# A channel-attention and dilated-attention kernel: softmax weights turned by TensorE, taps summed three at a time, attention loads cut to 32 rows

## The chip, the cores and the metric

One Trainium2 chip, one of its cores. The metric is the device time of the whole program in microseconds (us), as the median of the runs shown. About 0.3% is what a measurement of this kernel can tell from no change.

The engines are called as in the profile: PE (TensorE, matrix products), PEld (its weight loads), DVE (VectorE), ACT (ScalarE), POOL (GpSimd), SP (which here only issues transfers). POOL also issues transfers; those that add to their target in flight are all issued by POOL.

## The reference

The input x is 4 images of 192 channels of 128 x 128 pixels, in float32. Two layers follow each other.

```
# layer 0: attention between channels
qkvl = dwconv3x3(conv1x1(x, w_qkv), w_dw)            # 4 x 192 channels
q, k, v, l = split(qkvl, 4)                           # 8 heads of 24 channels
q, k = q / norm(q), k / norm(k)                       # over all pixels
attn = softmax(q @ k.T * temperature)                 # 24 x 24 for each head and image
out  = attn @ v
L    = silu(fc2(relu(fc1(mean(l)))))                  # one number for each channel
x    = conv1x1(L + out + x, w_proj) + L

# layer 1: attention between neighbouring pixels
x    = x + dwconv3x3(x, pos_w) + pos_b
q, k, v = conv1x1(x, qkv_w)                           # 3 groups of 64 channels, dilation 1, 2, 3
for g in groups:                                      # 2 heads of 32 channels in a group
    scores = q . k at the 9 dilated neighbours (reflected at the border)
    out[g] = softmax(scores / sqrt(32)) weighted sum of v at the 9 neighbours
y    = conv1x1(concat(out), proj_w)
```

## The kernel before, in words

The program has three stages. **Projection** (`project`) makes the q and k channels of layer 0, stores them to memory (`qk_dram`), and makes the convolved v (`v_dram`, `v2_dram`). **Channel attention** (`channel_attention`) reads q and k back row by row, convolves them on PE with banded 32 x 32 tap matrices and forms the small attention matrices, already multiplied with the projection (`mix1`, `mix2`). **The second pass** (`second_pass`) does the rest: it forms layer 0's output h, and from it the whole of layer 1.

Projection and second pass work in 64 blocks: pairs of images (2) by four rows of pixels (32). A tile is 128 partitions by `PX` = 512 pixels. In the second pass a block goes through these steps, with the names of the code:

- `h_product`, `h_evict` (L1081, L1085): h, 128 channels of each image, and the last 64 channels of both images in one tile; written into rings of 12 rows (`hboth`, `hring`).
- `centre`, `tap` (L1121, L1133): the 3 x 3 convolution of the first 128 channels, both images in one instruction of 1024 elements. The middle tap goes from ACT to a PSUM tile `pa`; DVE adds six taps (`SUMMED`). The other two (`MOVED`) are made by ACT (`moved`, L1146), added to each other and then to the tile `y` by two transfers that POOL issues (`moved_sum`, L1158). `moved` has one buffer.
- `side`, `side_rows`, `side_sum`: the same for the last 64 channels, by ACT, two adding transfers and POOL.
- `kv_product` (L1235, L1238), `kv_evict`: k and v, into rings for each dilation.
- `query` (L1292, L1295): q of one group, in one PSUM tile. Its second half is one matmul with a 128 x 128 block matrix (`wq2`).
- `prod` (L1303): DVE, q times k for three taps at once (1536 elements), nine in a block.
- `pick_sums` (L1314), `evicted_scores`, `by_pixel` (L1363): PE sums over channels, and turns the scores so that pixels lie on partitions.
- `top` to `part2` (L1366 to L1396): softmax, and the weights split into three bfloat16 parts that sum to float32.
- `weights` (L1401): a transposing transfer from SP brings them back to tap-on-partition, into `e_sb`.
- `expand` (L1436): PE spreads the weights of one tap over its 32 channels, a bfloat16 matmul of 108 rows with 512 columns, into a PSUM tile `ex` (two buffers); 27 in a block.
- `term` (L1442): DVE multiplies it with v; 27 in a block, of 512 elements.
- `term_sum` (L1445): POOL adds the terms; 24 in a block, of 512 elements.
- `out_product` (L1454, L1458), `out_evict`, `store`: the last projection. For channels 128 up it uses a 128 x 128 block matrix (`wo2`).

The order on every engine is fixed before the program runs. `Schedule` simulates the five engines and a sixth, DMA, with the cost that each `add` states; among the ready operations of an engine it takes the one of lowest rank, where rank is the block number plus a figure from `PLACES`. A change of the PE's tile shape (the `shape` of an `add`) costs `change` in the simulation and `change_rank` in the choice. `hold` says how many tiles of a kind may live at once. The engines run their queues in that order, waiting on semaphores.

In channel attention, SP and PE follow the order of the code. For each of 48 steps t (eight channels of a head) `Rows.load` has SP issue one load of small tap tables (`few`) and ten row loads of 64 or 32 partitions (`PIECES`); POOL then copies the taps into three banded matrices. `cut_taps` and `cut_loaded` load what is needed at the borders between 32-row strips, also on SP. The steps of `gates` (the L branch) are taken during head 0.

Of the kernel before, what the change touches and what calls it, by code (L numbers as in the profile page):

```python
# [29 lines left out]
NS = NG * NT * 4  # L30
GT = NT * 4
# [121 lines left out]
PIECES = (((0, 2), (2, 2)), ((0, 2), (2, 1), (3, 1)), ((0, 2), (2, 2)), ((0, 1), (1, 2), (3, 1)))  # L153
LAST = [(e, r, n) for e in range(4) for r, n in PIECES[e] if r + n == 4]
OTHERS = [(e, r, n) for e in range(4) for r, n in PIECES[e] if r + n < 4]


class Rows:
# [14 lines left out]
    def load_taps(self, t):  # L173
        first, j = self.place(t)
        few = self.few[t] = self.few_p.tile([STRIP, 4, 2, 3, STRIP], F32, tag="few", name=f"few{t}")
        self.nc.sync.dma_start(
            few.rearrange("p e c x m -> p e (c x m)"),
            self.bands_in[:, first : first + CH0]
            .rearrange("p (e c) x m -> p e (c x m)", e=4)[:, :, j * 3 * STRIP : (j + 2) * 3 * STRIP],
        )  # L180

    def spread_taps(self, t, i):

        band, few = self.bands[t % 3], self.few[t]
        group = slice(i * STRIP, (i + 1) * STRIP)
        self.nc.gpsimd.tensor_copy(band[group, :, :, :, 1 : STRIP - 1], few[:, :, :, :, 1 : STRIP - 1])  # L186
        for e, m in ((i, 0), ((i + 1) % 4, STRIP - 1)):
            self.nc.gpsimd.tensor_copy(band[group, e, :, :, m : m + 1], few[:, e, :, :, m : m + 1])  # L188
# [17 lines left out]
    def load(self, t):  # L206
        if t >= 6 * HEADS0:
            return
        self.load_taps(t)
        self.load_rows(t, OTHERS + LAST)  # L210
        for i in range(4):
            self.spread_taps(t, i)
# [49 lines left out]
def rows3(t):  # L262
# [10 lines left out]
SECOND = "wp1 wq1 wq2 wkv wkv2 wo wo2 posw posb pick order spread".split()  # L273
SUMMED, MOVED, TAPS = (0, 1, 2, 6, 7, 5), (3, 8), 0.075
# [58 lines left out]
    "loads": (0.5697, 0),  # L333
    "h_product0": (-0.8250, 0),
    "h_evict0": (0.7179, 0),
    "h_product1": (-0.2901, 0),
    "h_evict1": (4.5043, 0),
    "h_product2": (-0.7755, 0),
    "h_evict2": (-0.2139, 0),
    "centre": (5.7183, 0),  # L340
    "tap": (2.8884, 0.19030),
    "moved": (-0.0827, 0),
    "moved_sum0": (3.1492, 0),
    "moved_sum1": (4.7398, 0),
    "side1": (1.2593, 0.00003),
    "side0": (0.7171, 0.00011),
    "side_rows0": (2.1868, 0),
    "side2": (1.6271, 0.00019),
    "side_rows2": (1.4785, 0),
    "side_sum1": (10.8296, 0),  # L350
    "side_sum2": (5.4172, 0),
    "kv0": (1.7866, 0.00185),
    "kvev0": (-0.0330, 0.01478),
    "kv1": (3.2540, 0.00019),
    "kvev1": (-2.0029, 0),
    "kv2": (2.4499, 0),
    "kvev2": (1.1258, 0),
    "query0": (2.8659, 0),
    "prod0": (2.9696, 0),
    "query1": (3.3887, 0),  # L360
    "prod1": (3.0988, 0),
    "query2": (3.4244, 0),
    "prod2": (3.5942, 0),
    "pick0": (3.5728, 0.17857),
    "pick1": (3.9636, 0),
    "evicted_scores": (1.8388, 0),
    "by_pixel": (3.8163, 0),
    "top": (6.6680, 0),
    "below": (5.0643, 0),
    "exponential": (10.6231, 0),  # L370
    "total": (-2.1855, 0),
    "divide": (3.8560, 0),
    "part0": (-5.1709, 0),
    "rest": (-2.3314, 0),
    "part1": (-0.0711, 0),
    "part2": (1.6351, 0),
    "weights": (12.2563, 0),
    "expand": (4.2596, 0),
    "term": (4.7246, 0),
    "term_sum": (8.9696, 0),  # L380
    "out0": (6.1072, 0.00004),
    "outev0": (6.1953, 0),
    "store0": (18.8924, 0),
    "out1": (6.1208, 0),
    "outev1": (7.1247, 0),
    "store1": (9.7231, 0),
# [3 lines left out]
def channel_attention_then_dilated_attention(ctx: ExitStack, tc: tile.TileContext, d, out: bass.AP):  # L390
# [23 lines left out]
    with ExitStack() as early:  # L414
        band_p, u_p, few_p = (
            early.enter_context(tc.tile_pool(name=n, bufs=k)) for n, k in (("pab", 1), ("pau", 2), ("pax", 1))
        )
        rows = Rows(nc, d["bands"], qk_dram, few_p, band_p, u_p, lent)
        dwv = load(band_p, "dwv")
# [19 lines left out]
        project(tc, x, load, loads, dwv, sums, qk_dram, v_dram, v2_dram)  # L439
# [9 lines left out]
def project(tc, x, load, other_loads, dwv, sums, qk_dram, v_dram, v2_dram):  # L449
# [4 lines left out]
    with ExitStack() as ctx:  # L454
# [9 lines left out]
        plan_projection(nc, stage, x, wx, wx2, dwv, vboth, ring, sums, qk_dram, v_dram, v2_dram)  # L464
# [5 lines left out]
def plan_projection(nc, stage, x, wx, wx2, dwv, vboth, ring, sums, qk_dram, v_dram, v2_dram):  # L470
# [130 lines left out]
    load_ops, pairs = {}, {}  # L601

    def plan_products(n):
# [9 lines left out]
        for mt in range(4):  # L613
# [11 lines left out]
            hold("us", evs[0], add("SP", at(f"qkst{mt}", n), 0.3, (qk_store, n, mt), evs, latency=5.0))  # L625
# [47 lines left out]
    for n in range(2 * NB + 1):  # L673
        if n < 2 * NB:
            plan_products(n)
        if n >= 1:
            plan_conv(n - 1)

# [59 lines left out]
def channel_attention(tc, d, load, qk_dram, mix1, mix2, rows, gates):  # L738
# [7 lines left out]
    with ExitStack() as ctx:  # L746
        pool = lambda n, k, **kw: ctx.enter_context(tc.tile_pool(name=n, bufs=k, **kw))
# [6 lines left out]
        def bank(name, shape):  # L754
            taken.append(name)
            of = ps_x if len(taken) % 7 == 0 else ps_c
# [40 lines left out]
        def cut_taps(hd):  # L797
            taps = cut_p.tile([128, 2, 3, STRIP], F32, tag="taps", name=f"cuttaps{hd}")
            nc.sync.dma_start(taps, d["cuttaps"][:, hd])
            return taps  # L800

        def cut_loaded(hd, edge):
            u = cut_p.tile([128, 2, B * W], F32, tag=f"u{edge}", name=f"cut{hd}_{edge}")
            first = (edge + 1) * STRIP - 2
            for which in range(2):
                for h in range(2):
                    c0 = which * C + hd * CH0 + h * (CH0 // 2)
                    nc.sync.dma_start(
# [40 lines left out]
        def cut_squares(hd, edge, cut, sums):  # L849
            square = st.tile([128, B, 2, 2 * CH0], F32, tag="square", name=f"square{hd}_{edge}")  # L850
# [7 lines left out]
        def products(hd, q, sq, k, sk, us, taps):  # L858
# [3 lines left out]
            for b in range(B):  # L862
# [19 lines left out]
                if b == 1:  # L882
                    for edge in range(3):
                        cuts.append(cut_turned(hd, edge, s_cuts[edge]))
                        cut_squares(hd, edge, cuts[edge], (sq, sk))
# [75 lines left out]
        pending, mixes = [gate(ps_s) for gate in gates], []  # L961

        def step():
            while pending:
                try:
                    return next(pending[0])
                except StopIteration:
                    pending.pop(0)
# [5 lines left out]
        def head(hd):  # L974
# [7 lines left out]
            for _, n, dx in order:  # L982
# [10 lines left out]
                if n == 23:  # L993
                    taps = cut_taps(hd)
# [3 lines left out]
                if n % 4 == 3:  # L998
                    step()
                if n % CH0 == CH0 - 1:  # L1000
                    sums.append(squares(hd, which, stats[which]))
            products(hd, fulls[0], sums[0], fulls[1], sums[1], us, taps)
            pending.append(finish(hd))

        small, wph = {w: load(wts, w) for w in SMALL}, {}
        with tc.manual_schedule(engines={mybir.EngineType.PE, mybir.EngineType.SP}):
            for t in range(3):
                rows.load(t)
            for hd in range(HEADS0):
                head(hd)  # L1010
            load_mixing(HEADS0 - 1)
            while pending:
                step()
# [4 lines left out]
def second_pass(tc, x, w2, xv_p, mix1, mix2, biases, v_dram, v2_dram, out):  # L1018
# [4 lines left out]
    with ExitStack() as ctx:  # L1023
# [8 lines left out]
                xv=XV, y=3, y2=3, prod=4, middle=2, side=1, moved=1, term=4, acc=4, o=3, s_sb=1, e=2, mx=2, sm=2, e_sb=2,  # L1032
            ),
            dict(pc=2, ex=2, q=1, pa=1, sc=1),
            dict(xv=xv_p),
            (0.12, 1.6704),
# [4 lines left out]
        wp1, wq1, wq2, wkv, wkv2, wo, wo2, posw, posb, pick, order, spread = (w2[n] for n in SECOND)  # L1041
# [50 lines left out]
        def plan_h(n):  # L1092
# [5 lines left out]
            for m in range(3):  # L1098
                us, shape = (0.86, FULL) if m < 2 else (0.96, COLS)
# [18 lines left out]
        def centre(n):  # L1118
            at = n * RB % RING
            to, of = tile_of("pa", ("pa", n), (128, RB, 2, W)), hboth[:, at : at + RB, :, 1 : W + 1]  # L1120
            nc.scalar.activation(  # L1121
                by_row(to), by_row(of), AF.Identity, bias=posb[:, 0:1], scale=posw[:, 0, 4:5]
            )

        def tap(n, t, last):
# [536 lines left out]
```

## Time and profile before

| | |
|---|---|
| median of 3 runs | 4275.49 us (4273.98 to 4283.89) |
| the profiled execution | 4267.28 us, span 4265.5 us, mean granted clock 0.978 |
| busy in the span | PE 4034.2, DVE 3813.7, POOL 3418.5, ACT 2627.5 us |
| projection, from 0 to about 811 us | PE busy 100%, DVE 96%, ACT 95%, POOL 85% (100 to 200 us) |
| channel attention, about 811 to 1485 us | PE 83%, DVE 62%, ACT 40%, POOL 34% (900 to 1000 us) |
| second pass, 1485 to 4265 us | PE 99%, DVE 99%, POOL 94%, ACT 60% (2000 to 2100 us) |

The second pass is 65% of the span. A share of busy time is read within a stage: the same DVE that is 62% busy in the attention has no free time in the second pass. A PE that is "busy" is not PE at its peak, because its matmuls overlap and their ends are modelled; what a matmul costs is read from the distance between starts.

### The profile page before, as it was taken

To read this page: it belongs to the slowest core of one execution; us is meant where nothing else is said; L and a number is where in the kernel's file an instruction comes from. 1 tells how busy PE (TensorE), PEld (TensorE's weight loads), DVE (VectorE), ACT (ScalarE), POOL (GpSimd) and SP (SyncE) were. 2 spreads that over 40 slices of the span, in tenths; PEclk is the share of its full clock that TensorE was granted. 3 is DMA by queue.
4 is the path that set the end of the run, shared out by engine and by line. 5 is a ranking of instruction groups with operands and counts; after the bars stand their busy time and mean duration, and the time that the engine had idled before them with its cause. 6 is when DMAs were issued, how large, how long until landed. Compare 5 with 4: busy or idle time off the path is not lost.

```text
span 4265.5 us, 79212 instructions
## 1 busy us (share of the span) xinstructions
PE 4034.2 (95%) x28064; PEld 1611.7 (38%) x28064; DVE 3813.7 (89%) x5580; ACT 2627.5 (62%) x4882; POOL 3418.5 (80%) x3447
## 2 busy tenths in 40 slices
PE   8999999888888888999999999999999999999996
PEld 3333333355555522333333333333333333333331
DVE  6999999866576558999999999999999999999996
ACT  7999999744344375565565656655565656656531
POOL 6888888733433227999999999999999999999998
PEclk9999999899999999999999999999999999999997
DMA  8888888687978676566666666555555555555521
GB/s 249 266 269 255 264 272 277 201 188 178 197 185 188 145 179 120 125 137 127 129 126 133 127 133 133 122 133 128 130 124 134 130 132 133 128 130 128 116 48 33
DMA packets 479016, 677.12 MB, mean 159 GB/s; under 512 B 139508, under 2 KB 314416, under 8 KB 478620
## 3 DMA queue, kind: packets, MB, share of 16 engines
q1 hardware_dynamic: 439580, 504.71, 43.9%
q0 software_dynamic: 39040, 167.33, 21.3%
q8 instruction: 223, 3.65, 0.4%
q14 instruction: 173, 1.42, 0.1%
HBM read 278.08 MB, written 201.33 MB: 112 GB/s over the span
## 4 chain that ended last, share of the span: by engine, by line
PE 75%; DVE 13%; issue 6%; POOL 3%; ACT 1%; DMA 1%; SPq 0%; DVEq 0%; POOLq 0%; ACTq 0%
PE sc L1314 9%; PE ex L1436 8%; PE ph L1081 8%; PE pc L773 8%; PE pu L494 7%; PE pkv L1235 5%; DVE term L1442 4%; PE pkv L1238 4%; PE q L1295 4%; PE q L1292 4%; PE pu L499 4%; DVE prod L1303 3%; PE gram L876 3%; PE pu L645 2%; PE po L1458 2%
## 5 line engine op out<-in xcount | busy, mean ns | idle before, releaser
L1445 POOL TENSOR_TENSOR acc<-acc,term 128x512 f32<-128x512 f32 x1536 | 2037.8, 1332 | 143.7 <-DVE term L1442 57.4
L1442 DVE TENSOR_TENSOR term<-ex,vring 128x512 f32<-128x512 f32 (+2 forms) x1596 | 994.7, 658 | 55.9 <-PE ex L1436 43.1
L1303 DVE TENSOR_TENSOR prod<-q,kring 128x1536 f32<-128x1536 f32 (+1 forms) x600 | 1003.8, 1681 | 20.5 <-PE q L1292 10.7
L571 POOL TENSOR_TENSOR v_True<-v_True,side 128x512 f32<-128x512 f32 (+1 forms) x512 | 644.1, 1270 | 130.0 <-ACT side L560 98.9
L1436 PE MATMUL ex<-e_sb,spread 108*128 108x512 bf16 x1728 | 567.5, 387 | 50.8 <-DVE term L1442 31.1
L548 DVE SCALAR_TENSOR_TENSOR pa<-vboth,dwv,pa 128x1024 f32<-128x1024 f32 (+1 forms) x448 | 574.1, 1282 | 37.8 <-ACT pa L541 12.4
L1248 ACT COPY kring<-pkv 64x512 f32<-64x512 f32 x384 | 223.5, 582 | 415.8 <-PE pkv L1238 410.2
L1133 DVE SCALAR_TENSOR_TENSOR pa<-hboth,posw,pa 128x1024 f32<-128x1024 f32 (+1 forms) x320 | 407.2, 1273 | 38.8 <-ACT pa L1121 19.9
L1314 PE MATMUL sc<-prod,pick 128*32 128x512 f32 x3456 | 428.3, 598 | 1.8 <-DVE prod L1303 1.8
L1436 PEld LDWEIGHTS <-spread 108*128 108x128 bf16 x1728 | 133.3, 97 | 661.0 <-issue 642.9
L1461 ACT COPY o<-po 128x512 f32<-128x512 f32 x192 | 106.3, 588 | 445.1 <-PE po L1458 241.6
L1081 PE MATMUL ph<-lent,mix 128*64 128x512 f32 (+1 forms) x1024 | 375.0, 597 | 2.4 <-DMA mix<-mixed 2.4
L1235 PE MATMUL pkv<-y,wkv 128*128 128x512 f32 x768 | 364.1, 596 | 8.1 <-DMA y<-moved 7.9
L494 PE MATMUL pu<-xt,wx 128*128 128x512 f32 x768 | 355.6, 606 | 11.2 <-DMA xt<-in_x 7.5
L560 ACT ACTIVATE side<-ring,dwv 128x512 f32<-128x512 f32 (+1 forms) x512 | 347.5, 724 | 25.3 <-POOL v_True L571 21.2
L784 DVE BATCH_NORM_STATS2 stats<-conv 128x6 f32<-128x128 f32 x1536 | 306.6, 275 | 62.0 <-ACT conv L782 60.0
L1165 ACT ACTIVATE side<-hring,posw 128x512 f32<-128x512 f32 (+1 forms) x512 | 341.0, 710 | 8.6 <-DMA side<-side 6.5
L782 ACT COPY conv<-pc 128x512 f32<-128x512 f32 x384 | 226.9, 616 | 162.2 <-PE pc L773 153.0
L186 POOL COPY band<-few 32x720 f32<-32x720 f32 x192 | 151.6, 789 | 197.4 <-DMA few<-in_bands 166.5
L773 PE MATMUL pc<-u,band 32*32 32x508 f32 (+1 forms) x6144 | 263.9, 613 | 30.9 <-issue 30.0
L1248 ACT COPY vring<-pkv 64x512 f32<-64x512 f32 x384 | 224.1, 584 | 45.7 <-PE pkv L1238 32.8
L188 POOL COPY band<-few 32x6 f32<-32x6 f32 x384 | 70.6, 199 | 191.9 <-DMA few<-in_bands 101.5
(172 smaller groups left out, 6329.5 us busy)
## 6 DMA issues: line engine op xcount, KB each, us to landing
qk_dram<-us SPq DMA_DIRECT2D x192, 512.0 KB
side<-side POOLq DMA_DIRECT2D x124, 768.0 KB, 7.0
u<-qk_dram SPq DMA_DIRECT2D x192, 256.0 KB
xt<-in_x SPq DMA_DIRECT2D x64, 512.0 KB
v_dram<-v_False SPq DMA_DIRECT2D x64, 512.0 KB
lent<-in_x SPq DMA_DIRECT2D x128, 256.0 KB
lent<-v_dram SPq DMA_DIRECT2D x128, 256.0 KB
y<-moved POOLq DMA_DIRECT2D x64, 512.0 KB, 5.2
```

Source lines behind the costliest of these rows:

```text
L494: mm(pu, wx[:, mt * 128 : (mt + 1) * 128], tiles["xt", n][:, im, :], start=True, stop=False)
L548: nc.vector.scalar_tensor_tensor(by_row(to[:, o : o + length]), by_row(vboth[:, at : at + length, :, t % 3 : t % 3 + W]), dwv[:, 0, t : t ...
L571: nc.gpsimd.tensor_add(v[:, rows, :], v[:, rows, :], z[:, rows, :])
L773: nc.tensor.matmul(pc[r * STRIP : (r + 1) * STRIP, :, to], band[at, e, c, dx, :], u[at, e, c, :].rearrange("p (b w) -> p b w", w=W)[:, :, of],
L1081: mm(to, w[:, cols], tiles["xv", n, j, im], start=j == 0, stop=j == 2)
L1235: mm(rows3(tile_of("pc", key)), w, tiles["y", n, im], start=True, stop=False)
L1248: nc.scalar.copy(rows[HALVES[im], :, pad : pad + W], rows3(tiles["pkv", n, pair, im])[HALVES[e]])
L1303: nc.vector.tensor_mul(to[:, :, px].rearrange("p t (r w) -> p t r w", w=W), q.unsqueeze(1).to_broadcast([128, 3, *q.shape[1:]]), three,)
L1314: mm(sc[quad * 32 : (quad + 1) * 32, :], pick[:, QR - 4 * row : QR - 4 * row + 32], tiles["prod", n, k // NT, k % NT // 3][:, k % 3, :], s ...
L1436: mm(rows3(tile_of("ex", ("ex", n, g, t))), spread[:, t, :], e_sb, start=True, stop=True)
L1442: nc.vector.tensor_mul(rows3(to[:, px]), rows3(ex[:, px]), win)
L1445: nc.gpsimd.tensor_add(tiles["acc", n, g], tiles["acc", n, g], tiles.pop(("term", n, g, t)))
```

## The change

In the second pass:

- The weights are turned by PE in place of the transposing transfer: `turn` (24 bfloat16 matmuls of 128 columns in a block, in a `pa` tile) and `turned` (three ACT copies).
- The weights lie in two halves of the partitions, even taps in 0 to 59, odd taps in 64 to 111. An `expand` is three matmuls, of 60 and 48 rows, into one PSUM tile of three banks; there is one such tile.
- `term` handles three taps in one instruction of 1536 elements; `term_sum` adds two tiles of 1536 elements, then folds with two adds of 512.
- `centre` and `tap` go image by image (512 elements, `pa` of one bank); DVE adds five taps, not six; the third tap in `MOVED` is made by ACT after the first adding transfer, and there are three adding transfers.
- `wq2` and `wo2` are no block matrices any more: two 64 x 64 matmuls each.
- Softmax rows are ordered so that the nine taps lie side by side; the bfloat16 parts are interleaved. Buffers: `prod` 3 (was 4), `term` 2, `first` 2, `ex` 1, `e` 1, `parts` 1, `o` 2.
- `PLACES` and the change figures are new, so the order on every engine is new.

In channel attention: row loads of 32 partitions, sixteen for each step; tap tables and the border loads on POOL's queue, the tap tables one step ahead; POOL follows the order of the code; the first three steps' taps are made at the start of the program, and their rows are loaded in the projection's schedule as soon as the last q and k are stored; the first 14 PSUM tiles avoid the bank `ps_x`; the `gates` steps move from head 0 to later heads.

```diff
-PIECES = (((0, 2), (2, 2)), ((0, 2), (2, 1), (3, 1)), ((0, 2), (2, 2)), ((0, 1), (1, 2), (3, 1)))
...
+SINGLE = tuple(tuple((r, 1) for r in range(4)) for _ in range(4))
+PAIRED = (((0, 2), (2, 2)), ((0, 2), (2, 1), (3, 1)), ((0, 2), (2, 2)), ((0, 1), (1, 2), (3, 1)))
...
-        self.load_taps(t)
-        self.load_rows(t, OTHERS + LAST)
-        for i in range(4):
-            self.spread_taps(t, i)
+        if t == 3:
+            self.load_taps(t)
+        self.load_rows(t, [(e, r, n) for e in range(4) for r, n in SINGLE[e]])
+        if t + 1 < 6 * HEADS0:
+            self.load_taps(t + 1)
+        self.spread_taps(t, self.nc.gpsimd.tensor_copy)
...
-SUMMED, MOVED, TAPS = (0, 1, 2, 6, 7, 5), (3, 8), 0.075
+SUMMED, MOVED, TAP = (0, 1, 2, 7, 5), (3, 8, 6), 0.65
...
+        for t in range(3):
+            for e in range(4):
+                for r, n in (SINGLE if t else PAIRED)[e]:
+                    run = (ahead.load_rows, t, [(e, r, n)])
+                    stage.schedule.add("SP", -99 + t, 0.6, run, stored)
...
-            of = ps_x if len(taken) % 7 == 0 else ps_c
+            of = ps_x if len(taken) % 7 == 0 and len(taken) > 14 else ps_c
...
-                    nc.sync.dma_start(
+                    nc.gpsimd.dma_start(
                         u[h * G : h * G + 2 * CH0, which],
...
-                xv=XV, y=3, y2=3, prod=4, middle=2, side=1, moved=1, term=4, acc=4, o=3, s_sb=1, e=2, mx=2, sm=2, e_sb=2,
+                xv=XV, y=3, y2=3, prod=3, middle=2, side=1, moved=1, first=2, term=2, acc=4, o=2, s_sb=1, mx=2, sm=2, e_sb=2,
             ),
-            dict(pc=2, ex=2, q=1, pa=1, sc=1),
+            dict(pc=2, ex=1, q=1, pa=1, sc=1),
             dict(xv=xv_p),
-            (0.12, 1.6704),
+            (0.1, 4582.6473),
...
             for k, t in enumerate(MOVED):
-                mvs.append(add("ACT", at("moved", n, k), 1.15, (moved, n, k, t), mvs[-1:]))
+                mvs.append(add("ACT", at("moved", n, k), 1.15, (moved, n, k, t), (both if k == 2 else mvs)[-1:]))
                 for m in range(2):
                     read("h", m, n, t // 3 - 1, mvs[k])
-            both = summed_by_transfer(at("moved_sum0", n), 4.0, (moved_sum, n, 0), mvs)
-            both = summed_by_transfer(at("moved_sum1", n), 4.0, (moved_sum, n, 1), [both, two])
+                if k:
+                    after = [mvs[k], mvs[0], *both]
+                    both = [summed_by_transfer(at(f"moved_sum{k - 1}", n), 4.0, (moved_sum, n, k), after)]
+            both = summed_by_transfer(at("moved_sum2", n), 4.0, (moved_sum, n, 0), [*both, two])
             hold("moved", mvs[0], both)
...
-                mm(q, wq2[:, g, :], tiles["y", n, 2], start=False, stop=True)
+                for half in HALVES:
+                    mm(q[half], wq2[half, g, :], tiles["y", n, 2][half], start=False, stop=True)
...
-            e_sb = tile_of("e_sb", ("e_sb", n), (128, RB * NG, W), BF16)
-            nc.sync.dma_start_transpose(e_sb, parts[n % 2].rearrange("p r g c -> p (r g c)"))
+        def turn(n, i):
+            across = tile_of("pa", ("across", n, i), (128, 4, W))
+            for k in range(4):
+                of = parts[n % len(parts)][:, 4 * i + k].rearrange("p t s f -> p (t s f)")
+                for rows, cols in zip((slice(0, G), PARTED[1]), (slice(0, G), slice(60, 108))):
+                    mm(across[rows, k, :], of[:, cols], unit, start=True, stop=True)
+
+        def turned(n, i):
+            if i == 0:
+                tile_of("e_sb", ("e_sb", n), (128, nh, W), BF16)
+            rows = slice(0, PARTED[1].stop)
+            nc.scalar.copy(tiles["e_sb", n][rows, 4 * i : 4 * i + 4, :], tiles.pop(("across", n, i))[rows])
...
-        def expand(n, g, t):
-            e_sb = tiles["e_sb", n].rearrange("p (r g) w -> p r g w", g=NG)[:NS, :, g, :]
-            mm(rows3(tile_of("ex", ("ex", n, g, t))), spread[:, t, :], e_sb, start=True, stop=True)
+        def expand(n, g, ty):
+            ex = tile_of("ex", ("ex", n, g, ty), (128, 3, PX))
+            e_sb = tiles["e_sb", n].rearrange("p (r g) w -> p r g w", g=NG)[:, :, g, :]
+            for t in range(3 * ty, 3 * ty + 3):
+                half = PARTED[t % 2]
+                mm(rows3(ex[:, t % 3, :]), spread[half, t, :], e_sb[half], start=True, stop=True)
...
+        def term_sum(n, g, k):
+            add_to = nc.gpsimd.tensor_add
+            first = tiles["term", n, g, 0]
+            if k < 2:
+                add_to(first, first, tiles.pop(("term", n, g, k + 1)))
+            elif k == 2:
+                add_to(tile_of("acc", ("acc", n, g)), first[:, 0, :], first[:, 1, :])
+            else:
+                acc = tiles["acc", n, g]
+                add_to(acc, acc, tiles.pop(("term", n, g, 0))[:, 2, :])
...
-                mm(tiles["po", n, 1, 0], wo2[:, g, :], acc, start=g == 0, stop=g == NG - 1)
+                for half in HALVES:
+                    mm(tiles["po", n, 1, 0][half], wo2[half, g, :], acc[half], start=g == 0, stop=g == NG - 1)
```

## The prediction

> **What bounds the kernel now.** First the slices and the chain of the page (one digit is the busy tenths of 107 us):
>
> ```profile
> PE   8999999888888888999999999999999999999996
> ...
> DVE  6999999866576558999999999999999999999996
> ...
> POOL 6888888733433227999999999999999999999998
> ...
> PE 75%; DVE 13%; issue 6%; POOL 3%; ACT 1%; DMA 1%; SPq 0%; DVEq 0%; POOLq 0%; ACTq 0%
> ```
>
> From slice 17 on three engines are full at once, and the chain runs through PE. Then the timeline of SP's queue: the transposing transfer is issued once a block.
>
> ```profile
> 2019.59 1.45 SPq L1401 DMA_TRANSPOSE e_sb<-parts  x1
> ...
> 2186.29 1.47 SPq L1401 DMA_TRANSPOSE e_sb<-parts  x1
> ```
>
> Three others lie between, so a block takes 166.7 / 4 = 41.67 us. Over 1900 to 3900 us (48 blocks) the groups by shape say who fills that:
>
> ```profile
> L1445 POOL TENSOR_TENSOR acc<-acc,term 128x512 f32<-128x512 f32 x1154 | 1533.5, 1333 | 93.0 <-DVE term L1442 26.9 <-DVE acc L1442 7.1 <-PE ph L1081 1.8
> L1303 DVE TENSOR_TENSOR prod<-q,kring 128x1536 f32<-128x1536 f32 x426 | 741.8, 1745 | 2.0
> L1442 DVE TENSOR_TENSOR term<-ex,vring 128x512 f32<-128x512 f32 x1139 | 733.6, 677 | 26.7 <-PE ex L1436 25.9 <-POOL acc L1445 0.2
> L1436 PE MATMUL ex<-e_sb,spread 108*128 108x512 bf16 x1298 | 418.6, 382 | 12.7 <-DVE term L1442 12.4
> ```
>
> DVE instructions overlap the next by about 0.07 us (a term of 0.68 is followed after 0.60, a prod of 1.74 after 1.67). From start to start a block costs DVE 27 x 0.60 + 9 x 1.67 + 6 taps x 1.20 + softmax 2.4 = 40.9 us. POOL: 24 sums 31.1, two side sums 2.7, four issues 3.0, softmax 3.0, together 39.8. PE: the distances between starts fill 41.67, of which the profile shows only 0.4 as waiting: 41.3. So PE bounds, DVE is 2% behind, POOL 4%.
>
> **The change, part by part (us per block).** *DVE.* Nine terms of 1536 have the shape and the PSUM operand of L1303: 9 x 1.67 = 15.0 for 16.2 (bounds: 9 x 3 x 0.60, no gain, and 15.0). Ten taps of 512: L1133 takes 1.281 at 1024 and 1.011 at 768 elements, 0.74 at 512, less the overlap 0.67: 6.7 for 7.2 (bounds 6.0 and 7.4). The sum over taps reads them side by side: about 0.3 less (bounds 0 and 0.5). DVE 40.9 to 38.9.
>
> *POOL.* The projection's adds give the fixed part:
>
> ```profile
> L571 POOL TENSOR_TENSOR v_True<-v_True,side 128x512 f32<-128x512 f32 x488 | 617.1, 1277 | 116.7 <-ACT side L560 95.8 <-POOL v_True L571 0.3
> ...
> L571 POOL TENSOR_TENSOR v_True<-v_True,side 128x384 f32<-128x384 f32 x9 | 9.0, 1002 | 10.0 <-ACT v_True L541 9.1 <-ACT side L560 0.6
> ```
>
> 2.15 ns an element and 0.18 fixed; 1536 take 3.5, beside DVE (1333 against 1277) 3.6 (bounds 3.5, and 3 x 1.30 if nothing is saved). Six of these and six of 512: 29.4 for 31.1. One more issue +0.6, strided bfloat16 parts +0.3 (0 to 0.6). POOL 39.8 to 39.0.
>
> *PE.* Out go 27 expands of 0.246 (start to start): -6.6. In come nine triples; even and odd taps have separate rows and banks, so a triple takes two slots of 0.22: +4.0 (bounds: 3.8, and 6.6 if halves don't overlap). The turn is new: 24 bfloat16 matmuls of 128 columns; nearest row `st` (128 x 108 float32, one each 0.11) with pairs in column halves side by side: 1.3 (bounds 0.7 and 2.6). The 64 x 64 pairs replace a full matmul of 0.86 each at no cost, if they run together. Tile shapes:
>
> ```profile
> 2020.59 1.13 PE L1238 MATMUL pkv<-y,wkv 64*128 64x512 f32 x4
> 2021.65 2.78 PE L1314 MATMUL sc<-prod,pick 128*32 128x512 f32 x24
> ```
>
> One pair of row halves takes 1.06 to the next start; twelve such matmuls in one run (L1458, 2003.12 to 2005.90) take 2.78, so a further pair adds 0.86: entering and leaving a shape cost 0.2, 0.1 a change. Before there are 18 changes a block. Expand now leaves the full shape, and with one `ex` tile nine triples must stand apart; if other narrow work lies between them, 22 changes: +0.4 (bounds 16 and 30: -0.2 and +1.2). PE 41.3 - 6.6 + 4.0 + 1.3 + 0.4 = 40.4.
>
> Here a rule speaks against the change. The Trainium skill, "TensorEngine Tiling (Array Packing)", Restrictions and Gotchas, says that different row tiles cannot access the same PSUM bank simultaneously. The new halves of q and of the output do just that: six pairs would take 1.71 and not 0.86, +5.1, PE 45.5 and the program about 245 us slower. The trace has such pairs in the projection:
>
> ```profile
> 796.79 0.65 PE L509 MATMUL pu<-xt,wx 64*64 64x512 f32 x2
> 796.80 0.65 PE L509 MATMUL pu<-xs,wx 64*64 64x512 f32 x2
> ```
>
> The two of `xt` are two row halves into one bank; with the two of `xs` all start within 0.02 us (the second of the two passes of a float32 product follows 0.48 later). I take the row: no cost.
>
> *ACT* gets a third `moved` 1.15, three `turned` of 0.6, strided parts and exponential about 1.2, 0.15 for split centres: 25 becomes 29.3 of 41, covered unless ACT is held at the head of its queue. SP loses the transpose. A third adding transfer of 512 KB joins DMA engines that are 60% busy: covered.
>
> *Waits.* `ex` (one tile), `q`, `prod` (3), `term` (2) and `pa` tie PE, DVE and POOL together: PE must refill `ex` between two terms while DVE has a prod or two taps (1.3 to 1.7), and behind a blocked expand stand all PE products. DVE has 1.5 of slack under PE. I add 0.4 (bounds 0.1 and 1.5). Period 40.8, -0.9; times 64 = -56 us (range of the sum: 39.5 to 42.5).
>
> *Ramp of the second pass.* The chain in order of time has
>
> ```profile
> 1645.46 20.03 DMA e_sb<-parts
> ```
>
> With 9.36 at 1593.80 that is 29 us. The turn puts about 5 there, and the third adding transfer is late next, about +9: -15 (bounds 0 and -25).
>
> *Attention.* At its start PE stands, for DVE's last projection taps hold a PSUM bank:
>
> ```profile
> 840.25 3.08 PE L773 MATMUL pc<-lent,band 32*32 32x512 f32 x40 [15.56 <-DVE v_False L548]
> ```
>
> With 5.2 in three shorter gaps that is 20.8. The new bank rule removes the wait; then the rows are late: the last stores are issued at 812 and land about 5 later, three steps of 2.1 MB at 228 GB/s (860 to 880) take 27, the last one's products 8, so three steps end about 852; before, 867: -12 (bounds 0 and -20). Afterwards a head takes about 79 us and PE's gaps there are mostly "issue", at no buffer's end. 16 loads of about 0.5 us cost SP 8 of 13.2 us a step: hidden, though close. Twelve border loads and six tap loads a head cost POOL some 15 us of 79, at 35% busy: hidden; POOL's waits for `few` (263 us) end, but only 2 us of PE's waits point to POOL. Taken as 0 (bounds -15 and +25). The gate steps move but stay. The three steps' taps at the program's start precede ACT's first eviction at 16.85: 0 (up to +5).
>
> **Sum.** -56 - 15 - 12 = -83 on the span: 4265.5 to 4182. The profiled run was 8 us below the median, so the predicted median is 4190.
>
> **Rivals.**
> *1. The adding transfers bound a block (slower).* `moved` has one buffer, and now holds it over three transfers, the third tap being made only after the first:
>
> ```profile
> y<-moved POOLq DMA_DIRECT2D x48, 512.0 KB, 5.2
> moved<-moved POOLq DMA_DIRECT2D x47, 512.0 KB, 8.7
> ```
>
> 2 x 1.15 + 8.7 + 1.15 + 8.7 + 5.2 = 26. Each issue also waits in POOL's queue behind adds of up to 3.6, and ACT's third tap in ACT's queue: 31 to 36. It decides from 41.7; at 45 the program is 3.3 x 64 - 27 = 185 slower, 4460. For it: a late `y` stops PE at `kv_product`, with everything behind. Against it: 6 us of room.
> *2. PE gets nothing.* 30 changes and 0.8 of coupling: period 41.7, only ramp and attention remain, or are lost too: 4250 to 4290.
> *3. PE groups its shapes well,* 16 changes: PE 39.8, DVE 38.9, period 40.0 and -107 - 27: 4140, with the attention's gain 4100.
>
> **How the numbers follow.** The forecast (4150 to 4245) 0.47; rival 3 (below 4150) 0.22; rival 2 (4245 to 4295) 0.14, of it 0.06 within 0.3% (13 us) and 0.04 above; rival 1, or coupling worse than 1.5, 0.17. Faster 0.73, same 0.06, slower 0.21. The range 4090 to 4330 leaves out 0.05 below and 0.13 above.
>
> **What would show it.** A block period of 40.4 to 41.2; `term` near 1.67 apart, nine a block; POOL adds of 3.5; 20 to 24 shape changes; the 64 x 64 pairs starting together; `e_sb` gone from the chain; no 15 us gap at 840; heads of 79 us. Wrong if PE waits at expand or `kv_product` for more than 1.5 a block, if the turn costs over 2.5, or if heads lengthen because tap or border loads now queue on POOL.

## The result, and the profile after

| | before | after |
|---|---|---|
| median | 4275.49 us | 4301.66 us (4295.03 to 4302.51, 5 runs) |
| ratio, 95% interval | | 1.0054 (1.0036 to 1.0073) |
| the profiled execution, span | 4267.28, 4265.5 us | 4296.32, 4294.5 us |
| first product of h (end of the attention) | 1475.7 us | 1442.2 us |
| from there to the end | 2789.8 us | 2852.4 us |

The forecast was 4190. The change is slower by 0.5%, although its attention ends 33.5 us earlier: the second pass takes 62.6 us more. The slices and the chain of the page (one digit is now 107 us again):

```profile
PE   8999999899999788999999999999999999999995
...
DVE  6999999866867458899898899999999999999995
...
POOL 6888888754554227889788789999999999999998
...
PE 50%; DVE 10%; POOL 3%; issue 2%; ACT 1%; DMA 1%; POOLq 0%; DVEq 0%; ACTq 0%
```

In slices 17 to 24 POOL shows eights and sevens, and DVE eights among its nines, where before had only nines; behind them, up to the last slice, nothing is missing. PE's 50% of the chain must not be set beside the 75% of before: this chain can be followed back only to 1421 us, near the end of the attention, and its parts add up to 67%. Within the second pass PE has 64% of the chain from 1500 to 2500 us (71% before) and 88% from 2700 to 3600 us (80% before). The cause shows in a row that occurs once a block, the reciprocal of the softmax, picked from DVE's timeline:

```profile
1886.99 0.45 DVE L1413 RECIPROCAL sm<-sm 128x48 f32<-128x48 f32 x1
...
1928.88 0.45 DVE L1413 RECIPROCAL sm<-sm 128x48 f32<-128x48 f32 x1
...
1967.80 0.45 DVE L1413 RECIPROCAL sm<-sm 128x48 f32<-128x48 f32 x1
...
2024.53 0.45 DVE L1413 RECIPROCAL sm<-sm 128x48 f32<-128x48 f32 x1
...
2062.27 0.45 DVE L1413 RECIPROCAL sm<-sm 128x48 f32<-128x48 f32 x1
...
3014.59 0.45 DVE L1413 RECIPROCAL sm<-sm 128x48 f32<-128x48 f32 x1
...
3055.47 0.45 DVE L1413 RECIPROCAL sm<-sm 128x48 f32<-128x48 f32 x1
...
3096.22 0.45 DVE L1413 RECIPROCAL sm<-sm 128x48 f32<-128x48 f32 x1
```

The distances are 41.9, 38.9, 56.7, 37.7 in the early stretch and 40.9, 40.8 in the late one. Over all 63: the first 24 run 38.7, 53.6, 33.7, 58.6, 35.5, 40.1, 52.0, ... with a mean of 44.68; then they lie between 40.1 and 41.3, most at 40.7 or 40.8, until the last four. In the kernel before, the first 24 have a mean of 42.06 and the later ones, without the last four, 41.64. So the forecast period of 40.8 is there, but only from block 25 on. Busy time in one stretch of each kind (the pairs are busy us and instructions):

```profile
core 0: us, PE busy (x) PEld busy (x) DVE busy (x) ACT busy (x) POOL busy (x), PEclk, DMA share, GB/s
2000.00:2100.00 100.00, 88.11 (x417) 29.59 (x413) 79.43 (x66) 59.30 (x111) 82.97 (x48) 0.97 0.53 118
3000.00:3100.00 100.00, 99.91 (x509) 36.72 (x506) 97.20 (x89) 68.78 (x127) 92.97 (x56) 1.00 0.61 139
```

In the early stretch PE, DVE, ACT, POOL and the transfers all do less. No engine has become the bound; they wait for each other. The waits of 1700 to 2600 us (us in total, times, longest):

```profile
POOL term L1498 <- DVE term L1492: 75.5, 50, 4.0
...
DVE term L1492 <- PE ex L1484: 53.5, 42, 3.1
...
PE ex L1484 <- DVE term L1492: 20.6, 21, 2.7
```

and of 2700 to 3600 us, equally long:

```profile
POOL term L1498 <- DVE term L1492: 38.0, 25, 2.1
...
DVE term L1492 <- PE ex L1484: 17.7, 24, 0.9
```

Over the buffer `ex` PE waits for DVE in the first stretch only, and DVE waits for PE three times as long there. The groups of the late stretch (2700 to 3515 us, by shape) hold the sizes that the prediction named:

```profile
L1498 POOL TENSOR_TENSOR term<-term,term 128x1536 f32<-128x1536 f32 x120 | 422.1, 3517 | 37.7 <-DVE term L1492 34.8
L1492 DVE TENSOR_TENSOR term<-ex,vring 128x1536 f32<-128x1536 f32 x175 | 305.5, 1746 | 15.3 <-PE ex L1484 14.7
L1341 DVE TENSOR_TENSOR prod<-q,kring 128x1536 f32<-128x1536 f32 x174 | 299.6, 1749 | 7.4 <-PE sc L1352 7.4
```

A term of 1536 takes what a prod takes, 1.75 us, and a POOL add of 1536 takes 3.52 (forecast 3.5 to 3.6).

### The profile page after: what moved, and what is told of

Same layout as the page of the kernel before. It is cut to its first block, busy times and chain, and to the rows that moved or that the text cites. A ratio compares the mean times of both kernels' runs of the same rounds, so it can differ in the third digit from the quotient of the medians.

```text
span 4294.5 us, 80521 instructions
## 1 busy us (share of the span) xinstructions
PE 4079.7 (95%) x30368; PEld 1617.5 (38%) x30368; DVE 3721.7 (87%) x4648; ACT 2870.0 (67%) x5215; POOL 3433.9 (80%) x2869
## 4 chain that ended last, share of the span: by engine, by line
PE 50%; DVE 10%; POOL 3%; issue 2%; ACT 1%; DMA 1%; POOLq 0%; DVEq 0%; ACTq 0%
PE ph L1109 10%; PE sc L1352 7%; PE pkv L1272 7%; PE ex L1484 5%; PE q L1330 4%; DVE prod L1341 4%; PE q L1333 4%; DVE term L1492 4%; PE pkv L1275 3%; PE po L1513 3%; PE po L1517 3%; POOL term L1498 2%; DVE pa L1164 1%; PE st L1398 1%; PE across L1437 1%
## 5 line engine op out<-in xcount | busy, mean ns | idle before, releaser
L1498 POOL TENSOR_TENSOR term<-term,term 128x1536 f32<-128x1536 f32 x384 | 1350.3, 3517 | 170.3 <-DVE term L1492 161.8
L1492 DVE TENSOR_TENSOR term<-ex,vring 128x1536 f32<-128x1536 f32 (+1 forms) x600 | 1008.3, 1684 | 126.4 <-PE ex L1484 120.7
L1352 PE MATMUL sc<-prod,pick 128*32 128x512 f32 x3456 | 457.8, 602 | 6.4 <-DVE prod L1341 3.1
L1164 DVE SCALAR_TENSOR_TENSOR pa<-hboth,posw,pa 128x512 f32<-128x512 f32 (+1 forms) x512 | 382.1, 746 | 56.4 <-ACT pa L1148 34.9
L1484 PE MATMUL ex<-e_sb,spread 60*128 60x512 bf16 (+1 forms) x1728 | 353.0, 389 | 62.1 <-DVE term L1492 57.8
L1196 ACT ACTIVATE side<-hring,posw 128x512 f32<-128x512 f32 x512 | 345.3, 712 | 27.8 <-DMA side<-side 24.8
L797 PE MATMUL pc<-u,band 32*32 32x508 f32 (+1 forms) x6144 | 313.3, 631 | 11.7 <-DMA u<-qk_dram 7.8
L1500 POOL TENSOR_TENSOR acc<-term 128x512 f32<-128x512 f32 x192 | 275.9, 1437 | 16.1 <-PE po L1513 14.8
L1503 POOL TENSOR_TENSOR acc<-acc,term 128x512 f32<-128x512 f32 x192 | 260.6, 1358 | 10.4
L1484 PEld LDWEIGHTS <-spread 60*128 60x128 bf16 (+1 forms) x1728 | 78.4, 94 | 446.1 <-issue 393.9
## 6 DMA issues: line engine op xcount, KB each, us to landing
u<-qk_dram SPq DMA_DIRECT2D x512, 128.0 KB
```

What stands on the lines that cost most here:

```text
L1164: nc.vector.scalar_tensor_tensor(to[:, o : o + length], hboth[:, at : at + length, im, t % 3 : t % 3 + W], posw[:, 0, t : t + 1], acc[:, o ...
L1352: mm(sc[quad * 32 : (quad + 1) * 32, :], pick[:, QR - 4 * row : QR - 4 * row + 32], tiles["prod", n, k // NT, k % NT // 3][:, k % 3, :], s ...
L1484: mm(rows3(ex[:, t % 3, :]), spread[half, t, :], e_sb[half], start=True, stop=True)
L1492: nc.vector.tensor_mul(by_row3(to), by_row3(ex), three)
L1498: add_to(first, first, tiles.pop(("term", n, g, k + 1)))
```

## The experiments

None of the kernels leaves out any part of the computation. Times of the attention are given per head, as the mean of seven distances between the ends of heads (the reciprocal of k's norms, once a head): before 77.6 us, after 75.5. Profiles with the same attention (after, e1, e2, e3, e4, e7) give 74.6 to 75.8, so about 1 us a head is what one profile can't tell. e2, e3 and e7 ran once each.

**Theory A: the order.** Costs and waits of a block are as forecast; the order that `Schedule` writes out is irregular for 24 blocks. Its own plan, made with the costs in the code, has distances of 37.9, 50.2, 34.7, 56.7, 35.0, 39.3, 53.7 at the start, much as the chip shows them, and ends the second pass at 2812 us where the plan of before ends at 2765. **Theory B:** contention on the chip that the plan does not know, from the third adding transfer or the smaller buffers; then another order of the same operations would not help.

**e1_steady.** Each operation's rank becomes its block number plus its place in blocks 32 to 52 of the changed kernel's own plan (a table, `STEADY`), with no price on a change of shape in the choice; operations, tiles, buffers and costs stay.

```diff
+        steady(stage.schedule.ops)
+        stage.schedule.change_rank = 0.0
         stage.run(tc)
```

> The changed kernel with one edit: the second pass takes the order that its own plan settles into from block 25 on (for every operation its place within a block, read from the plan's blocks 32 to 52) for all 64 blocks. Operations, tiles, buffers and costs are the same. Theory A (the loss is in the written-out order of the first 24 blocks): the irregular intervals of 34 to 58 us vanish, every interval is near 40.7 us, the second pass is about 80 us shorter, the program near 4220 us, 1.3% below the kernel before. Theory B (the new parts with their single buffers are disturbed on the chip until the pipeline has settled, whatever the order): the first blocks stay irregular and the time near 4300 us. Theory C (the third adding transfer holds the block in the first half): as B.

Measured: 4211.05 us, ratio 0.9854 (0.9838 to 0.9870). The same stretch of its windows as above, and the once-a-block row:

```profile
2000.00:2100.00 100.00, 100.00 (x509) 36.77 (x505) 97.04 (x82) 67.16 (x124) 93.19 (x57) 1.00 0.62 145
```

```profile
1888.41 0.45 DVE L1583 RECIPROCAL sm<-sm 128x48 f32<-128x48 f32 x1
...
1929.16 0.45 DVE L1583 RECIPROCAL sm<-sm 128x48 f32<-128x48 f32 x1
...
1969.91 0.46 DVE L1583 RECIPROCAL sm<-sm 128x48 f32<-128x48 f32 x1
```

From the fifth distance on it is about 40.75 (40.1 to 41.3, without the last four), with the same operations, costs and buffers. A holds, and B falls. The second pass is 86 us shorter than after's (81 by the plan); the other 6 of the span's 92 lie in the attention, which is the same code. Why the planner's own choice takes 24 blocks to settle is not shown: e1's order starts from an empty pipeline too, so that alone is not the reason.

**e2_rank6, e3_rank3.** One figure of the planner, the price of a change of tile shape in its choice; 6.0 in e2, 3.0 in e3.

```diff
-            (0.1, 4582.6473),
+            (0.1, 6.0),
```

> The changed kernel with one number changed: the penalty by which the planner avoids a change of the tile shape is 6 blocks in place of 4583. The planned order then settles after 18 blocks, not 24, and its planned end is 25 us earlier. Theory A: about 25 us faster than the changed kernel, near 4275 us. Theories B and C: near 4300 us.

> The changed kernel with the same number at 3 blocks. The planned order then never settles (planned intervals from 31 to 64 us throughout) and ends 131 us later than the plan of the changed kernel. Theory A: about 130 us slower than the changed kernel, near 4430 us, with irregular intervals to the end. Theories B and C: the second half keeps its 40.7 us, near 4300 us.

Measured: 4272.45 and 4425.94 us. In e3 the distances stay irregular to the end. Three values of one figure, with not one instruction added, give 4272 to 4426 us: the order alone moves the time by more than the 85 us that were forecast for the whole change. The second pass is 27 us shorter in e2 than in after and 135 us longer in e3, where the plans say 25 and 131.

**e4_attn_new.** The changed projection and attention with the second pass of before.

```diff
-SUMMED, MOVED, TAP = (0, 1, 2, 7, 5), (3, 8, 6), 0.65
+SUMMED, MOVED = (0, 1, 2, 6, 7, 5), (3, 8)
...
```

> The kernel before's second pass behind the changed projection and attention. If the stages add up as the two profiles show (first h product at 1442 in place of 1476 us), 33 us faster than before: near 4242 us. If the earlier end of the attention is given back in the second pass (loads not yet there, an engine late), less than 15 us faster.

Measured: 4231.58, ratio 0.9896 (0.9881 to 0.9911). The attention's gain is real, and stays by itself: first product of h at 1446.8, second pass 2785.7 with a ramp (first product of h to first reciprocal) of 111.6 us.

**e5_pairs, e6_sptaps.** Two of the edits to the attention are tried in turn on e1: the loads of 32 partitions (undone in e5, the first lines), and the queue of tap tables and border loads (SP again in e6, the last lines, and so for `few` and `cut`).

```diff
-        self.load_rows(t, [(e, r, n) for e in range(4) for r, n in SINGLE[e]])
+        self.load_rows(t, [(e, r, n) for e in range(4) for r, n in PAIRED[e]])
...
-            nc.gpsimd.dma_start(taps, d["cuttaps"][:, hd])
+            nc.sync.dma_start(taps, d["cuttaps"][:, hd])
```

> The kernel of e1 with row loads of 64 partitions again (the list of ten loads a step, as before the change); all else as e1. If the 32-row loads shorten the heads (75 us each in e1, 78 before), heads go back to 77 or 78 and the time to about 4230 us; if the tables' and border loads' own queue does it, heads stay at 75 and the time at 4211 us.

> The kernel of e1 with the tap tables and the border loads of the attention issued by SP again, tap tables still one step ahead; all else as e1. If leaving SP's queue is what shortens the heads, they go back to 77 or 78 us (4230 us); if the 32-row loads do it, they stay at 75 (4211 us).

Measured: e5 4269.51, ratio 0.9997 (0.9981 to 1.0014); e6 4185.11, ratio 0.9795 (0.9749 to 0.9841). Neither came as expected: undoing the first edit lengthens a head by 8.6 us, more than the change had gained, and undoing the second shortens it by 3.7. So one edit gains and the other loses.

**e7_fewer.** Blocks 0 and 1 go back to two adding transfers and six taps on DVE, to see if the third transfer makes the ramp long.

```diff
+                summed = SUMMED[:3] + MOVED[2:] + SUMMED[3:] if n in FEWER else SUMMED
...
-            for k, t in enumerate(MOVED):
+            for k, t in enumerate(MOVED[:2] if n in FEWER else MOVED):
```

> The kernel of e1, but in the first two blocks DVE adds six taps and only two adding transfers follow, as before the change; the other 62 blocks as in e1. If the third transfer is what lengthens the ramp (128 us from the first h product to the first softmax sum in e1, 111 before), the ramp shrinks by 10 to 17 us, to about 4197 us. If the ramp is long because the order puts ACT's and PE's work for later blocks first, it shrinks by less than 5.

Measured: 4212.65. The first k and v product comes 45.8 us after the first of h (53.1 in e1, 45.7 before), but the first reciprocal 128.0 (128.4 in e1, 111.2 before). In this order the third transfer delays its own step and not the first softmax.

**e8_pairs_sp, e9_whole_sp.** The fourth corner of e1, e5 and e6: both edits undone; and e6 with loads of up to 128 partitions, seven a step (e9, shown).

```diff
+WHOLE = (((0, 4),), ((0, 3), (3, 1)), ((0, 2), (2, 2)), ((0, 1), (1, 3)))
...
-        self.load_rows(t, [(e, r, n) for e in range(4) for r, n in SINGLE[e]])
+        self.load_rows(t, [(e, r, n) for e in range(4) for r, n in WHOLE[e]])
```

> The fourth corner: 64-row loads and tap tables and border loads on SP, as before the change, with all else as e1. So far a head takes 75 us (32 rows, POOL's queue, e1), 83 (64 rows, POOL's queue, e5), 71 (32 rows, SP's queue, e6). If the two edits add, heads take 78 to 79 us, as in the kernel before, and the program about 4236 us. If 64-row loads hurt only beside POOL's transfers, heads stay near 72 us, 4190 us.

> The kernel of e6 with row loads of up to 128 partitions (seven a step). If what a large load costs is that PE's instruction fetches and other small transfers queue behind its packets, heads get longer with the size of a load: more than 80 us, with more issue gaps of PE that have a fetch in flight. If only the wrong grain of waiting mattered (a 64-row load waits for two strips), 128 rows cost a little more again, without gaps named issue.

Measured: e8 4217.74, ratio 0.9860 (0.9804 to 0.9915); e9 4254.28, ratio 0.9951 (0.9937 to 0.9966). Per head:

| rows loaded by | tap tables and border loads on POOL | on SP |
|---|---|---|
| 32 partitions | 74.6 (e1) | 70.9 (e6) |
| 64 partitions | 83.2 (e5) | 77.2 (e8) |
| up to 128 | | 81.2 (e9) |

Loads of 32 in place of 64 partitions gain 6 to 9 us a head; POOL's queue costs 4 to 6. With both undone (e8) a head takes 77.2 us for before's 77.6, so the other edits to the attention move the later heads by nothing that can be measured. The gain of the small loads shows in the waits of PE's weight loads from 900 to 1400 us, here of e1

```profile
PEld pc L967 <- issue: 41.5, 107, 2.6
```

and of e5, where only the loads' size differs:

```profile
PEld pc L967 <- issue: 128.9, 146, 6.0
```

In these gaps PE stands without any wait that the profile knows. From 900 to 1400 us PE and its weight loads stand together in this way, for over 0.25 us each, 40 times in e5 (78 us), 44 times before (70), 37 in e8 (56) and 38 in e9 (69), but 6 times in e1 (7) and 4 in e6 (2). PE's busy time is 68 us a head in both e6 and e9, so the 10 us between their heads are lost in the stands and not to the granted clock, which is lower in e9 (0.92 for 0.99).

What ends a stand can be read from the DMA packets. Queue q8 carries the instructions, 16 KB at a time. Of the 189 such stands in before, after, e1, e5, e6, e8, e9 and e10, 187 end 1.2 to 1.8 us after an instruction fetch has ended; of the 131 other stands of PE only 17 do. Nine tenths of the instructions recorded in this stretch are PE's. By this timing PE stands there for its next instructions. The fetch itself is not slower (1.2 us in e5 as in e1), and it is in flight for only 21 of e5's 78 us: it comes late. That large row loads hold it up before it starts fits the time lost, which grows with the loads (2, 56 and 69 us in e6, e8 and e9), as e9's expectation had it; what holds it up was not tried.

**e10_border_sp.** Which of the two transfers costs on POOL? Of e6's edits only the border loads and their tap table go back to SP; the tap tables `few` stay on POOL.

```diff
-                    nc.gpsimd.dma_start(
+                    nc.sync.dma_start(
                         u[h * G : h * G + 2 * CH0, which],
```

> The kernel of e1 with only the border loads and their table back on SP's queue; the tap tables stay on POOL's. If the border loads (12 issues a head on POOL, each about 1 us) are what costs 4 us a head, heads take 71 us and the program about 4185 us; if the tap tables do, 75 us and 4211 us.

Measured: 4166.99, ratio 0.9741 (0.9690 to 0.9792), 69.8 us a head. So the border loads are the cost, 4.8 us a head; tap tables on POOL cost nothing (e10's heads are 1.1 us shorter than e6's, no more than what one profile can't tell; the ratios' intervals overlap).

**e11_spin.** Why do they cost? Either they hold POOL's queue, for some 9 us ahead of the tap copies, as e1's timeline of POOL shows:

```profile
1016.02 0.57 POOL L993 DMA_DIRECT2D cuttaps<-in_cuttaps  x1
1016.59 3.83 POOL L1002 DMA_DIRECT2D cut<-qk_dram  x7
1021.75 0.54 POOL L1002 DMA_DIRECT2D cut<-qk_dram  x1 [1.34 <-DMA cuttaps<-in_cuttaps]
1023.24 2.13 POOL L1002 DMA_DIRECT2D cut<-qk_dram  x4 [0.94 <-ACT conv L976]
...
1026.38 0.77 POOL L190 COPY band<-few 32x720 f32<-32x720 f32 x1
```

(theory Q), or the transfers themselves are in the way (theory R). Work without any transfer, put in the same place of e10, tells these apart.

```diff
                     us = {edge: cut_loaded(hd, edge) for edge in range(3)}
+                    spin = cut_p.tile([128, 256], F32, tag="spin", name=f"spin{hd}")
+                    nc.gpsimd.memset(spin, 0.0)
+                    for _ in range(12):
+                        nc.gpsimd.tensor_add(spin, spin, spin)
```

> The kernel of e10 (new second pass in the repeated order; border loads on SP, tap tables on POOL) with some 9 us of work added to POOL's queue once a head, at the place where the border loads stood in e1: a scratch tile is cleared and added to itself twelve times (256 elements each). Nothing of the computation is left out. Theory Q: border loads on POOL cost 4.8 us a head because twelve issues and their waits hold POOL's queue for 9 us ahead of the tap copies that PE needs; the added work then costs the same, heads go from 69.8 to about 74.5 us and the program from 4167 to about 4200 us. Theory R: they cost because a second queue brings their 1.15 MB a head in among the row loads that PE waits for, ahead of rows issued before them, while on SP they follow those rows; POOL's 9 us are then hidden, heads stay at 69.5 to 70.5 us and the program at 4165 to 4175 us.

Measured: 4171.32, ratio 0.9750 (0.9716 to 0.9784), 69.9 us a head, with POOL held for 8.6 us. Q falls. For R, a window of e1 in which the border loads are issued (by POOL, from 1016.6 to 1025.4)

```profile
1016.00:1032.00 16.00, 14.76 (x274) 7.24 (x249) 13.19 (x69) 6.93 (x12) 12.41 (x28) 1.00 1.03 239
```

and one of e10 (by SP, from 1021.2 to 1031.5):

```profile
1016.00:1032.00 16.00, 15.44 (x332) 8.63 (x309) 13.75 (x72) 8.98 (x16) 8.34 (x24) 1.00 0.60 171
```

The DMA engines are full in e1 (share 1.03) and not in e10 (0.60). Twelve loads of 96 KB at 239 GB/s take 4.9 us, about what a head loses. PE waits longer for its rows, from 900 to 1400 us of e1

```profile
PEld pc L967 <- DMA u<-qk_dram: 36.1, 42, 2.0
```

and of e10

```profile
PEld pc L967 <- DMA u<-qk_dram: 22.9, 45, 1.8
```

And the waits of SP's queue in the same stretch, of e1

```profile
SPq L211 <- PE pc L967: 117.8, 99, 15.3
```

and of e10

```profile
SPq L211 <- PE pc L967: 32.2, 64, 2.2
```

say what is different about SP: in e1 its row loads pause once a head, for 11 to 15 us (from 983.6 to 995.0, for example), until PE gives row buffers back, and the DMA engines then have almost nothing to do (share 0.02 from 988 to 992). In e10 there is no such pause. So on SP the border loads come behind the rows that PE needs first, and take time in which the row loads would pause; on POOL's queue they move among those rows, and the pause stays empty. e11 shows that POOL's time is not the cause; this account of the transfers is read from the traces and was not tried by itself.

**e12_best.** e10 with an order of the same operations whose planned end lies 17.6 us earlier.

```diff
-    "loads 0 0": -1.49604,
...
```

> The kernel of e10 with other figures in the table of places: the same operations in an order whose planned end is 17.6 us earlier (2713.5 for 2731.1 us in the plan of the second pass; ramp -0.8, the first 24 intervals -6.4, the other 39 -8.5, drain -2.0). Theory A (the chip follows the planned order): about 4167 - 17 = 4150 us, 4142 to 4160, with a second pass of 2750 us for 2767. Rival: the plan is followed only roughly, and differences below one per cent are lost in waits that it does not know: 4162 to 4172 us.

Measured: 4151.20 us (4147.39 to 4154.13), ratio 0.9701 (0.9674 to 0.9729), the best of all; second pass 2747.3 us for e10's 2767.4, 20.1 earlier for the planned 17.6. In five orders of the same operations (e12, e1, e2, after, e3) the plan ends the second pass at 2713, 2731, 2787, 2812 and 2944 us, and the chip took 2747, 2767, 2826, 2852 and 2988: always 34 to 44 us more. So the plan foretold which order is better; the trouble was the order, not an error of the plan.

## Why the prediction was wrong, point by point

Differences from before on the profiled span, in us:

| step of the prediction | forecast | after | e1, the repeated order |
|---|---|---|---|
| period, 64 blocks | -56 | first 24 distances +63, other 39 -26 | -33, -15 |
| ramp of the second pass (first product of h to first reciprocal) | -15 | +21 | +17 |
| drain (not named) | 0 | +4 | +8 |
| start of the attention | -12 | -18 | -19 |
| rest of the attention | 0 | -15 | -21 |
| sum | -83 | +29 | -63 |

- **"Period 40.8, -0.9; times 64 = -56 us" is the step that failed, in its factor 64.** The settled period is 40.75, and PE does bound there: it is busy 99.9% of the time and shows no wait. But a new order on every engine need not be periodic from the first block, and 24 distances at 44.68 for 40.75 lose 94 us. The prediction put the new order at nothing and says no word of the plan, although the plan of the changed kernel ends the second pass 47 us later than that of before, and can be computed without the chip. It took the coupling (0.4, bounds 0.1 and 1.5) as the same in each block; the first 24 are 3.9 longer than the rest.
- **The 40.8 itself was met in part by luck.** Prods and terms of 1536 start 1.67 before the next DVE instruction (forecast 1.67), with 0.09 of wait for `ex` before each term, and POOL's adds take 3.52. On PE, from start to start, the triples of expand cost 3.85 us a block (forecast 4.0) and the turn 1.06 (1.3), but the other rows 0.7 more than forecast, with 25 changes of shape for 22. So PE's work is 40.7 for the forecast 40.4, and the 0.4 of waiting that made up the difference is not there.
- **Ramp: the gain of the turn came, but behind the first softmax; that the way to it grows was missed.** The two waits for the transposing transfer (29 us, at 1593.80 and 1645.46) lie behind the first reciprocal of before:

```profile
1586.96 0.45 DVE L1378 RECIPROCAL sm<-sm 128x48 f32<-128x48 f32 x1
```

Their gain falls into the first two distances: 51.9 and 44.5 before, 36.3 and 42.6 in e1, which is 17.5 less and stands in the row of the period. What the prediction had at nothing is the way to the first softmax: from the first prod to the first reciprocal it takes 58 us before, 69 after, 68 in e1. The 9 us counted for the third transfer are there (the first k and v product comes 55.4 us after the first h, for 45.7), but without it softmax starts no earlier (e7). The plan has the same lengthening (103 us from the first h before, 127 after, 124 in e1), so it comes from the order and the costs in it; which operation sets it stays open.
- **Start of the attention: about right,** with -18 for -12, though the -18 are taken at the end of the first head and hold what the other edits do to that head. The 15 us gap at 840 is gone; PE's longest stands there are 4.3 and 4.1 us for row loads.
- **"Rest of the attention, taken as 0"** was a gain of some 7 and a loss of some 5 us a head, both of which the prediction had at nothing. Smaller loads ended most of PE's "issue" gaps, which the prediction had seen and left without a cause (by their timing PE stands for its instructions, see e8 and e9). The sentence "twelve border loads and six tap loads a head cost POOL some 15 us of 79, at 35% busy: hidden" was right on POOL's time (e11) and overlooked what the transfers do to the rows.
- **What the repeated order leaves.** In e1 the second pass gains 23 us where 71 were forecast. The 57 distances in the middle give -46 and the first two -17.5, about as forecast; but the way to the first softmax costs 17, of which only the 9 of the third transfer had been counted, and the end of the pass, which the prediction did not name, costs 23 (the last four distances 15, the drain 8). That e1's 4211.05 us lies inside the forecast range all the same is luck: the attention gives -40 for -12.
- **The 64 x 64 pairs run side by side,** as taken from the projection's row, against the rule that the prediction quotes; here the measurement decides. In PE's timeline of after the three pairs of the output (four records each) take no more than the three pairs of the 64-row halves into two banks:

```profile
3043.01 2.74 PE L1513 MATMUL po<-acc,wo 64*64 64x512 f32 x12
...
3051.57 2.95 PE L1517 MATMUL po<-acc,wo 64*128 64x512 f32 x12
```

- **Rivals.** None came as described. Rival 1 is refuted by the landings of the adding transfers from 1700 to 2600 us, which are faster than before's 8.7 and as fast as its 5.2:

```profile
moved<-moved POOLq DMA_DIRECT2D x40, 512.0 KB, 4.8
y<-moved POOLq DMA_DIRECT2D x20, 512.0 KB, 5.3
```

The settled period of 40.75 says the same. Rival 2 came nearest in time (4290 at its top), but for another reason. The missing rival was a planned order that does not settle, for which before's own trace had a sign: its first distances are 51.9, 44.5, 42.1, 40.8, 39.4, and the stretch from which the period was read lay behind them.

## What to carry to other kernels

A period times the number of blocks assumes that the order is periodic: list the distances of a once-a-block row over the whole stage first, and where all engines grow idler together, ask the order, not an engine. When a change brings a new order, forecast the order as a term of its own; where a planner in the kernel writes the order, run it before the chip does and compare the two planned ends. A transfer moved to an idle engine's queue is not hidden by that engine's idleness; it can now move ahead of the transfers that it used to follow.

## What the runs showed of the hardware that was not expected

- Row loads of 4 KB a partition gave heads of 71, 77 and 81 us for 32, 64 and up to 128 partitions a load, with the same bytes, all issued by SP. The difference lies in PE's "issue" gaps, 187 of 189 of which end 1.2 to 1.8 us after an instruction fetch.
- 8.6 us of added POOL work a head cost nothing that can be measured (69.9 for 69.8 us), while 1.15 MB of transfers a head, moved to another queue, cost 4.8.
- The same operations with the same buffers, in four orders (e1, e2, after, e3), took 4211, 4272, 4302 and 4426 us.
